# An attention pair's last residual: its bias added in the scores, the sum made by accumulating transfers, and the next layer norm's sums and loads issued in other places

## The chip, the cores and the metric

The kernel runs on one core of one Trainium2 chip. The metric is the device time of one execution in microseconds (us). Everything is float32.

The core has an engine for matrix products (TensorE, "PE" in the profile, with its weight loads as "PEld"), VectorE ("DVE"), ScalarE ("ACT"), GpSimd ("POOL") and SyncE ("SP"). Each takes its own instructions in order. In this kernel SP issues the ordinary loads and stores, and POOL issues the transfers that add to what stands at their destination.

## The reference

The input x is (8, 512, 32, 32): eight batches of 512 channels by 1024 tokens. Two attention layers follow each other.

```python
# layer 0, tokens x channels
xn  = layer_norm(x_flat)                       # over the 512 channels
q, k, v = xn @ Wq.T + bq, xn @ Wk.T + bk, xn @ Wv.T + bv     # 8 heads of 64
out = softmax(q k^T / 8) v
x   = out @ Wo.T + bo + residual
# layer 1, channels x tokens
h   = group_norm(x)                            # 32 groups
q, k, v = wq h + bq, wk h + bk, wv h + bv      # one head of 512
o   = v softmax(q^T k / sqrt(512))^T
return x + (wp o + bp)
```

The change concerns the last line, and the layer norm of a later batch.

## The kernel before, in words

**Batches.** The loop over b = 0 to 7 does, for each batch, layer 0's eight heads (two matmul kinds, s and acc, for each pair of heads), its output product (x_out), layer 1's group norm, layer 1's attention, and then the projections k and q of the next batch's layer 0. The work on batches overlaps: while layer 1 of batch b runs, the sums of the layer norm of batch b+2 are made, and its values are loaded. So batches 6 and 7 have no such work. In the trace a batch takes 352.5 us.

**Layer 1.** Its weights are multiplied together once at the start. With "a" (from wq and wk) one projection qa replaces queries and keys, and with "m" (from wv and wp) the projection vm gives the merged values: the product of vm and the attention weights is already the output wp o. What is left of the biases of values and output is one column for each block of 128 output channels, `bm`.

**Products.** A 2 x 2 block product is done in seven steps instead of eight (`STEPS`, class `Product`). The operands of the steps are blocks such as `11` or `22` and sums of blocks (S1 to S4 of one side, T1 to T4 of the other, made on DVE). Each step multiplies into one of three accumulators in PSUM, called x, y and z. After steps 0, 2 and 3 ACT copies an accumulator out (`copy`, with `plain_shift` L464: tiles u(0, 0), u(0, 1), u(1, 1)), and matmuls may go on in the same accumulator only when that copy is done. After steps 1, 4 and 5 DVE adds an accumulator to the copied tile (`out`, L347). After the last step, number 6, ACT copies the whole block (1, 0). The scores have four such units of 128 keys in their two groups, the projections and the value product two, `r` = 0 and 1. In the profile, s, o, vm and so on name the product: `x_o<-T_p,vm` is a matmul of the value product into x.

**Side work.** Work that isn't tied to one step is queued with `later(...)` in a deque, `side`. Every step of a product ends with `tick`, which takes one piece from it and issues that piece's instructions on whatever engine they need; `until(lambda: not side)` issues all that is left. `nothing` is an empty piece. The order of instructions on PE, ACT, DVE and POOL is therefore fixed by the order in which the program is written out (`manual_schedule(engines=ORDERED)`). SP's loads and stores stand in program order as well, each waiting for its tile. Tiles come from pools that go round: 46 of 128 x 1024 (`big`), 9 of 128 x 512 (`half`), three double banks and two single banks of PSUM.

**Layer 1 of a batch, in order.**
- Group norm gives h1 from x1, layer 0's output. Right after it the four blocks of x1 are stored to DRAM (`put_away`, tiles x_away, 512 KB each), which frees their tiles.
- Projection qa, then the scores: four units. Of each block ACT takes the exponential (L945). DVE adds the exponentials up over the keys (`key_sums`, L968 and L970) and makes the sums of blocks for the value product (`operands`, L981; T3 of the second half is the third of four).
- `fold` adds partitions together by POOL's accumulating transfers: `halve` (L532) adds the upper half of the partitions to the lower, and four small ones (L528) bring them to 32 rows. The result is fold1.
- Projection vm (two units), and load of the weights w_k of the next batch.
- The value product, `Whole.values`. With its first step come, in the program, `ln.sums()` of `LayerNorm(b + 2)` and `inverse` (DVE L536 and others, ACT copies, DVE: 1 / sums, as `rden`).
- After each finished block of this product, `after(i, k)` does: DVE multiplies it by `rden` (L1045), DVE adds the bias column and the stored x1 in one instruction (L1046, `scalar_tensor_tensor`), SP stores the result in out (L1047). The stored x1 comes back in halves, tiles x1r of 128 x 512, 256 KB each, loaded by SP one step ahead (L1041). The very last block of the last batch is done in two halves (`halves`, with its own L1058 that adds the bias to the loaded x1).
- After unit 0 of the value product SP is given the four loads of x for batch b+2 (`load_x`, L152, 512 KB each), and `ln.queue()` puts the rest of that layer norm in the deque, a piece at a time.
- After unit 1: loads of w_q, loads of the stored values v_again, and the projections of k and q.

**The layer norm's sums.** `ln.sums()` brings in the four channel blocks of x with one copying and three accumulating transfers on POOL (L565, tile lns, 512 KB each), then a halve and four folds (L532 and L528, tile fold_mu). The first piece that `ln.queue()` put in the deque is `folded_means`: a transpose of fold_mu on DVE (L536, tile foldm), a reduction (L537) and a scaling (L602). After it come copies on ACT, `expand` (L522), and the centring of x (L629).

The lines at issue, in the program's order:

```python
            o_units[0].step(1)
            ln = LayerNorm(b + 2) if b + 2 < B else None
            if ln:
                ln.sums()
            whole.inverse()
            ...
            o_units[0].rest()
            if ln:
                ln.xt = load_x(b + 2)
                ln.queue()
            o_units[1].rest()
```

## Time and profile before

The median of 3 runs is 2888.99 us (2888.18 to 2889.49). One execution was profiled.

| | |
|---|---|
| profiled execution | 2889.16 us, span 2887.4 us, TensorE clock granted 0.999 |
| PE busy | 2870.4 us, 99% of the span |
| PEld busy (beside PE) | 1386.7 us, 48% |
| DVE busy | 1698.0 us, 59% |
| ACT busy | 1084.2 us, 38% |
| POOL busy | 345.2 us, 12% |
| moved by DMA | 277.17 MB; queue of SP 20.3% of 16 engines' time, queue of POOL 13.2% |
| loads x1r (SP) | 63 of 256 KB, 2.8 us from issue to landing |
| stores x_away (SP) | 32 of 512 KB |
| loads of x (SP) | 32 of 512 KB, 9.5 us |
| lns from x (POOL) | 24 of 512 KB, 5.3 us |
| halving of lns (POOL) | 6 of 256 KB, 8.4 us |
| fold_mu (POOL) | 24 of 64 KB, 2.9 us |
| halving and folds of the pairs' and layer 1's sums (POOL) | 78 of 256 KB, 3.4 us; 312 of 64 KB, 2.4 us |

The span is what the profiler saw, from the first instruction to the last; the time of the execution has 1.8 us more around it. A line of a timeline has the start in us from the beginning of the span, the busy time in us, the engine, the line of the kernel, the operation and its tiles, and in brackets the idle time of the engine before it and what ended that. SPq and POOLq stand for the issue of a DMA by these engines. A group's row has its count, its busy time and the mean of one in ns. Small DMA issues occupy their engine for some 0.8 us each on POOL, and the transfer itself then runs on its own.

### The profile page before, as it was taken

To read this page: it belongs to the slowest core of one execution; us is meant where nothing else is said; L and a number is where in the kernel's file an instruction comes from. 1 tells how busy PE (TensorE), PEld (TensorE's weight loads), DVE (VectorE), ACT (ScalarE), POOL (GpSimd) and SP (SyncE) were. 2 spreads that over 40 slices of the span, in tenths; PEclk is the share of its full clock that TensorE was granted. 3 is DMA by queue.
4 is the path that set the end of the run, shared out by engine and by line. 5 is a ranking of instruction groups with operands and counts; after the bars stand their busy time and mean duration, and the time that the engine had idled before them with its cause. 6 is when DMAs were issued, how large, how long until landed. Compare 5 with 4: busy or idle time off the path is not lost.

```text
span 2887.4 us, 27282 instructions
## 1 busy us (share of the span) xinstructions
PE 2870.4 (99%) x9695; PEld 1386.7 (48%) x9695; DVE 1698.0 (59%) x2181; ACT 1084.2 (38%) x1867; POOL 345.2 (12%) x507
## 2 busy tenths in 40 slices
PE   9999999999999999999999999999999999999998
PEld 4535454355543554445543455434554345543345
DVE  6667354774557645575456755568455674427734
ACT  4462224612256122651226512264222732226331
POOL 2020011200112011120111201011010110002000
PEclk9999999999999999999999999999999999999999
DMA  8134152341613326133252323423244231402302
GB/s 318 45 72 142 34 161 74 68 142 40 181 46 73 135 55 171 44 74 131 63 163 49 88 112 79 148 69 79 102 113 139 63 104 57 124 30 62 117 8 67
DMA packets 110129, 277.17 MB, mean 96 GB/s; under 512 B 16304, under 2 KB 20704, under 8 KB 109984
## 3 DMA queue, kind: packets, MB, share of 16 engines
q1 hardware_dynamic: 81760, 204.51, 20.3%
q0 software_dynamic: 28128, 70.81, 13.2%
q8 instruction: 78, 1.28, 0.2%
q14 instruction: 67, 0.55, 0.1%
q10 hardware_dynamic: 96, 0.02, 0.0%
HBM read 168.85 MB, written 59.24 MB: 79 GB/s over the span
## 4 chain that ended last, share of the span: by engine, by line
PE 99%; DMA 0%; DVE 0%; ACT 0%; issue 0%; SPq 0%; DVEq 0%
PE s L807 15%; PE acc L825 15%; PE x_s L451 8%; PE x_o L459 7%; PE x_v L443 4%; PE x_vm L443 4%; PE x_q L434 4%; PE x_k L434 4%; PE y_s L451 4%; PE x_qa L434 4%; PE x_out L434 4%; PE y_o L459 4%; PE y_v L443 2%; PE y_vm L443 2%; PE y_out L434 2%; PE z_s L451 2%
## 5 line engine op out<-in xcount | busy, mean ns | idle before, releaser
L816 DVE TENSOR_TENSOR sum<-sum,p 128x1024 f32<-128x1024 f32 x384 | 470.4, 1225 | 39.4 <-DVE sum L816 0.9
L810 ACT ACTIVATE p<-s 128x1024 f32<-128x1024 f32 (+1 forms) x608 | 478.8, 990 | 14.4 <-PE s L807 14.4
L807 PE MATMUL s<-q,k 64*128 64x512 f32 x2048 | 448.1, 592 | 0.0
L825 PE MATMUL acc<-p,v_again 128*64 128x512 f32 x1792 | 390.9, 594 | 0.0
L807 PEld LDWEIGHTS s<-q,k 64*128 64x128 f32 x2048 | 195.1, 186 | 251.6 <-issue 158.4
L532 POOL DMA_DIRECT2D sum<-sum x78 | 64.0, 821 | 1719.7 <-DVE sum L970 985.8
L825 PEld LDWEIGHTS acc<-p,v_again 128*64 128x64 f32 x1792 | 126.1, 137 | 261.3 <-issue 238.4
L528 POOL DMA_DIRECT2D fold<-sum x312 | 207.9, 757 | 328.5 <-DMA sum<-sum 199.8
L814 DVE TENSOR_TENSOR sum<-p,p 128x1024 f32<-128x1024 f32 x64 | 78.2, 1222 | 193.6 <-ACT p L810 193.6
L451 PE MATMUL x_s<-S_qa,T_gn 128*128 128x512 f32 x256 | 120.3, 592 | 0.0
L829 ACT COPY o<-acc 128x512 f32<-128x512 f32 x63 | 36.9, 585 | 221.3 <-PE acc L825 221.1
L459 PE MATMUL x_o<-T_p,S_vm 128*128 128x512 f32 x256 | 115.3, 593 | 0.2 <-ACT u(0, 1)_o L464 0.2
L347 DVE TENSOR_TENSOR p<-u(1, 1)_s,x_s 128x512 f32<-128x512 f32 x32 | 22.0, 688 | 128.8 <-PE x_s L451 128.8
L443 PE MATMUL x_vm<-w_m,T_gn 128*128 128x256 f32 x384 | 90.7, 379 | 0.0
L434 PE MATMUL x_qa<-T_gn,w_a 128*128 128x512 f32 x192 | 89.4, 594 | 0.8 <-ACT qa L477 0.8
L434 PE MATMUL x_out<-T_o,w_o 128*128 128x512 f32 x192 | 89.2, 594 | 0.0
L945 ACT ACTIVATE p<-p 128x512 f32<-128x512 f32 x96 | 60.3, 628 | 60.3 <-DVE p L347 60.3
L443 PE MATMUL x_v<-w_v,T_h 128*128 128x256 f32 x336 | 80.0, 381 | 0.0
L464 ACT COPY u(0, 0)_v<-x_v 128x512 f32<-128x512 f32 x16 | 9.4, 585 | 187.5 <-PE x_v L443 187.5
L434 PE MATMUL x_k<-T_h,w_k 128*128 128x512 f32 x168 | 78.9, 592 | 0.0
L434 PE MATMUL x_q<-T_h,w_q 128*128 128x512 f32 x168 | 78.9, 592 | 0.0
L451 PEld LDWEIGHTS x_s<-S_qa,T_gn 128*128 128x128 f32 x256 | 48.6, 190 | 61.2 <-issue 61.0
(334 smaller groups left out, 4252.1 us busy)
## 6 DMA issues: line engine op xcount, KB each, us to landing
sum<-sum POOLq DMA_DIRECT2D x78, 256.0 KB, 3.4
fold<-sum POOLq DMA_DIRECT2D x312, 64.0 KB, 2.4
x<-in_x_dram SPq DMA_DIRECT2D x32, 512.0 KB, 9.5
xr<-in_x_dram SPq DMA_DIRECT2D x64, 256.0 KB, 2.6
x_away<-x SPq DMA_DIRECT2D x32, 512.0 KB
x1r<-x_away SPq DMA_DIRECT2D x63, 256.0 KB, 2.8
v_away<-v SPq DMA_DIRECT2D x28, 512.0 KB, 2.6
v_again<-v_away SPq DMA_DIRECT2D x28, 512.0 KB, 6.5
```

What stands on the lines that cost most here:

```text
L434: nc.tensor.matmul(dst, a[:, k, ts(r, P)], b[:, k, :], start=(opens and k == 0), stop=(k == 1), skip_group_check=True)
L443: nc.tensor.matmul(dst[:, ts(m, CB)], b[:, k, ts(2 * r + m, P)], a[:, k, :], start=(opens and m == 0 and k == 0), stop=(k == 1), skip_grou ...
L451: nc.tensor.matmul(dst, b[:, k, ts(r, P)], a[:, k, :], start=(opens and k == 0), stop=(k == 1), skip_group_check=True)
L459: nc.tensor.matmul(dst, a[:, m, ts(r, P)], b[m // 2][:, m % 2, :], start=(opens and m == 0), stop=(m == NM // 2 - 1), skip_group_check=True)
L528: nc.gpsimd.dma_start(out=f[ts(q + i, BL), :], in_=t[ts(n, BL), ts(i, HB)], accum_op=ALU.add if n else ALU.bypass)
L532: nc.gpsimd.dma_start(out=t[:D, :], in_=t[D:, :], accum_op=ALU.add)
L807: nc.tensor.matmul(parts[i], self.k[m // 4][r, ts(m % 4, P)], self.q[r, :], start=True, stop=True)
L810: nc.scalar.activation(dst, src, AF.Exp, scale=1.0 / float(D) ** 0.5)
L814: nc.vector.tensor_add(self.sum, self.p[0], p)
L816: nc.vector.tensor_add(self.sum, self.sum, p)
L825: nc.tensor.matmul(acc[i * D : (i + 1) * D, :], value_of(self.vt, m, self.c * P + i * D, D), self.p[m][:, ts(i, HB)], start=(m == 0), stop ...
L945: nc.scalar.activation(p, s, AF.Exp, scale=float(C) ** -0.5)
```

## The change

- The bias is added to x1 ahead of its storage: `residual(i, k)` does two activations on ACT (identity with the bias column) on a block of x1, in place, and then SP stores it in x_away. The four pieces are put in the deque behind `query_sums`, so they come at the first steps of the scores, and not right after the group norm.
- For batches 0 to 6, `after(i, k)` has no load x1r and no `scalar_tensor_tensor`: behind the multiplication by `rden`, POOL issues a transfer that adds the stored half block to the tile (256 KB), and SP's store follows that. The last batch still loads x1r and adds it with a plain `tensor_add`, and the last block's L1058 is gone.
- `ln.sums()` is called behind unit 0 of the projection vm, after all that was left in the deque, and ahead of unit 1.
- `load_x(b + 2)` is called behind the first step of the value product and `inverse`.
- `ln.queue()` is called behind the second step of unit 1 and with it two empty pieces; the rest of both units comes after it. Before, it was called when unit 0 was complete.

```diff
@@ -1022,6 +1022,7 @@
 
         def values(self, v):
             b = self.b
+            more = b + 1 < B
             w = {f"{i + 1}{j + 1}": v[i, j].rearrange("p (m o) -> p m o", o=CB) for i in range(2) for j in range(2)}
             shared = {}
 
@@ -1034,16 +1035,19 @@
                     return y[i, k]
 
                 def ahead(n):
-                    if n + 1 not in BLOCK_OF or u.last and n == 5:
+                    if more or n + 1 not in BLOCK_OF or u.last and n == 5:
                         return
                     i, k = BLOCK_OF[n + 1]
                     xr = xr_of[i, k] = half_tile(f"x1r_{b}_{k}_{2 * i + r}")
                     nc.sync.dma_start(out=xr, in_=self.x1[i, k][:, ts(r, HB)])
 
                 def after(i, k):
-                    t, oc, xr = dest(i, k), 2 * i + r, xr_of[i, k]
+                    t, oc = dest(i, k), 2 * i + r
                     nc.vector.tensor_mul(t, t, self.rden[:, ts(k, HB)])
-                    nc.vector.scalar_tensor_tensor(t, t, bm[:, oc : oc + 1], xr, ALU.add, ALU.add)
+                    if more:
+                        nc.gpsimd.dma_start(out=t, in_=self.x1[i, k][:, ts(r, HB)], accum_op=ALU.add)
+                    else:
+                        nc.vector.tensor_add(t, t, xr_of[i, k])
                     nc.sync.dma_start(out=out[b, ts(oc, P), ts(k, HB)], in_=t)
 
                 u = Product(f"o1_{b}_{r}", w, self.p, value_part(r), plain_shift, dest,
@@ -1055,7 +1059,6 @@
                     oc = 2 + r
                     xr = half_tile(f"x1r_{b}_last")
                     nc.sync.dma_start(out=xr, in_=self.x1[1, 0][:, ts(r, HB)])
-                    nc.vector.tensor_scalar(xr, xr, bm[:, oc : oc + 1], None, ALU.add)
                     t = half_tile(f"y_{b}_last")
                     yield
                     both = (slice(0, HB // 2), slice(HB // 2, HB))
@@ -1246,7 +1249,15 @@
                 for n, _ in enumerate(gn.part(slice(None))):
                     meanwhile(n)
             h1 = gn.h
-            x1_away = {ik: put_away(wide(t), f"x1_away_{b}_{ik[0]}{ik[1]}") for ik, t in x1.items()}
+            x1_away = {ik: dram.tile([P, S], F32, tag=f"x1_away_{b}_{ik[0]}{ik[1]}", name=f"x1_away_{b}_{ik[0]}{ik[1]}")
+                       for ik in x1}
+
+            def residual(i, k):
+                t = x1[i, k]
+                for r in range(2):
+                    oc = 2 * i + r
+                    nc.scalar.activation(t[:, r, :], t[:, r, :], AF.Identity, bias=bm[:, oc : oc + 1])
+                nc.sync.dma_start(out=x1_away[i, k], in_=wide(t))
             h1b = operands(h1)
             if more:
                 add_operands(h1b)
@@ -1272,6 +1283,7 @@
             whole = Whole(b, qa, h1b, x1_away)
             s_units = whole.scores()
             whole.query_sums()
+            later(*(lambda ik=ik: residual(*ik) for ik in x1))
             for u in s_units[:2]:
                 u.step(2)
             for u in s_units[:2]:
@@ -1284,26 +1296,29 @@
             later(whole.fold)
             whole.operands(1)
             v_units, vm = project_v(f"vm{b}", wm_now, h1b)
-            for u in v_units:
-                u.rest()
+            v_units[0].rest()
+            ln = LayerNorm(b + 2) if b + 2 < B else None
+            if ln:
+                until(lambda: not side)
+                ln.sums()
+            v_units[1].rest()
             if more:
                 wk_next = load_w("k", b + 1)
             o_units = whole.values(vm)
             check = iter(()) if more else all_checks()
             o_units[0].step(1)
-            ln = LayerNorm(b + 2) if b + 2 < B else None
+            whole.inverse()
             if ln:
-                ln.sums()
-            whole.inverse()
+                ln.xt = load_x(b + 2)
             o_units[0].step(1)
             next(check, None)
             o_units[1].step(2)
             next(check, None)
-            o_units[0].rest()
             if ln:
-                ln.xt = load_x(b + 2)
+                later(*[nothing] * 2)
                 ln.queue()
-            o_units[1].rest()
+            for u in o_units:
+                u.rest()
             if more:
                 wq_next = load_w("q", b + 1)
                 vts = {ik: big_tile(f"v{b + 1}_again_{ik[0]}{ik[1]}") for ik in vn_away}
```

The order of the matmuls is the same in both programs, and so is the order of POOL's transfers apart from the added ones: layer 1's fold stood ahead of the layer norm's sums before, and still does.

## The prediction

> **What bounds the kernel now.** I read the shares of the span and the chain that ended last, then what TensorE waited for, then the timelines of POOL, SP, DVE and TensorE in one batch (batch 3; the program repeats every 352.5 us, eight times). From the page:

> ```profile
> PE 2870.4 (99%) x9695; PEld 1386.7 (48%) x9695; DVE 1698.0 (59%) x2181; ACT 1084.2 (38%) x1867; POOL 345.2 (12%) x507
> ...
> PE 99%; DMA 0%; DVE 0%; ACT 0%; issue 0%; SPq 0%; DVEq 0%
> ```

> TensorE is both the busy engine and the chain. The waits of TensorE (us in total, times, longest):

> ```profile
> PE pst_q L263 <- DMA w_q<-in_L_conv_wq_dram: 5.0, 2, 4.7
> PE pst_k L263 <- DMA w_k<-in_L_conv_wk_dram: 1.2, 1, 1.2
> PE x_qa L434 <- ACT gn L767: 0.8, 1, 0.8
> ...
> PE x_o L459 <- ACT u(0, 1)_o L464: 0.2, 1, 0.2
> ```

> After the first 15 us it waits about 3 us in the whole run. Nothing taken from DVE, ACT or SP can buy more than that, so the question is only whether the change makes a new wait. The timeline of POOL in batch 3 (start, busy, instruction, idle time before it and its releaser) has the chain of the layer norm's sums:

> ```profile
> 1431.11 1.16 POOL L565 DMA_DIRECT2D lns<-in_x_dram  x1
> 1435.70 0.87 POOL L565 DMA_DIRECT2D lns<-in_x_dram  x1 [3.44 <-DMA lns<-in_x_dram]
> ...
> 1452.84 0.82 POOL L532 DMA_DIRECT2D lns<-lns  x1 [4.73 <-DMA lns<-in_x_dram]
> 1462.03 1.05 POOL L528 DMA_DIRECT2D fold_mu<-lns  x2 [8.37 <-DMA lns<-lns]
> 1465.83 1.61 POOL L528 DMA_DIRECT2D fold_mu<-lns  x2 [2.75 <-DMA fold_mu<-lns]
> ```

> Each step waits for the landing of the one before. The 8.37 us is the interesting figure: the halving collided with the loads of x, issued by SP just before it:

> ```profile
> 1449.73 2.81 SPq L152 DMA_DIRECT2D x<-in_x_dram  x4
> ```

> The consumer on DVE, and the matmuls that stand beside it:

> ```profile
> 1462.83 0.69 DVE L347 TENSOR_TENSOR u(1, 1)_o<-u(1, 1)_o,x_o 128x512 f32<-128x512 f32 x1 [8.10 <-PE x_o L459]
> ...
> 1471.64 0.70 DVE L536 STREAM_TRANSPOSE foldm<-fold_mu 64x512 f32<-64x512 f32 x1
> ```

> ```profile
> 1462.56 3.60 PE L459 MATMUL y_o<-p,S_vm 128*128 128x512 f32 x8
> 1465.99 3.60 PE L459 MATMUL x_o<-T_p,vm 128*128 128x512 f32 x8
> ```

> Today foldm runs at 1471.64 without waiting, when all of unit 0 is done. The add at 1462.83 reads x_o, and the last step of unit 0 (1465.99) writes on into x_o, so it must wait for that add.

> [...] The trace has 687 ns from PSUM (L477) and 806 ns from SBUF (L767); I use the trace.

> **The change, part by part.**

> *Residual on ACT.* 8 activations a batch, 64 in all: by L767's 806 ns alone, about 0.72 us each back to back (four of L661 in 2.93 us), 46 us on an engine with 62% idle. They stand among the evacuations of the first score unit. In batch 3: copy u(0,1)_s 1375.07, exp p 1375.55 to 1376.08, then two residuals to 1377.5, then copy u(1,1)_s, which began at 1376.84, now 1377.5 to 1378.1. TensorE's next y_s step starts at 1378.30, its weights half a microsecond before. So 0.1 us a batch, between 0 and 0.4: 0.8 us in eight batches (0 to 3). The other four residuals end near 1381.0, before the exp of x_s due at 1381.94. The four x_away stores move from about 1335 to 1377 to 1382; their first readers on POOL come 80 us later, and what reuses the x buffers comes from 1424. SP's w_k loads behind them are needed at 1486.6. Nothing.

> *DVE.* 56 instructions L1046 at 0.752 us go (42 us), 7 shrink, one L1058 (0.48 us) goes: none is on the chain, so zero gain. SP loses 56 loads x1r of 256 KB; also hidden.

> *Accumulating transfers.* 56 issues on POOL at about 0.8 us (45 us on an engine with 88% idle). They stand behind the four fold_mu, so the first two outputs wait until about 1465. SP's stores wait for them, and behind the stores w_q and v_again. The last ones are ready at 1488.1, plus 0.8 to issue and 3 to land: v_again goes out near 1492.5, not 1489.4, w_q near 1485.5 and 1489; with up to 7 us to land they stand by 1500, and are needed at 1510.6 (x_q) and 1548.8 (acc). The output tiles live longer in the pool of nine half tiles: copy u(0,0) of k (1488.5) needs the store of the second output, gone by about 1475. Nothing, with 10 us of cover.

> *Sums and loads of x.* POOL's order is unchanged: the sums already follow the fold of layer 1, so they start no earlier. What moves is the loads of x, from 1449.7 to behind w_k: the first waits for T3 of p (DVE, 1427.9), the third for a fold, so all four go out between 1428 and 1430.5, just ahead of the first lns. And foldm moves up on DVE, ahead of the add at 1462.83. **DVE now stops at foldm until fold_mu has landed, with that add queued behind it, and TensorE waits for the add.**

> When does fold_mu land? lns to halving 21.7 (1431.11 to 1452.84). The halving and the four folds will be free of x; their price is that of a pair's sums:

> ```profile
> 1556.51 0.80 POOL L532 DMA_DIRECT2D sum<-sum  x1 [1.18 <-DVE sum L816]
> 1560.20 1.06 POOL L528 DMA_DIRECT2D fold<-sum  x2 [2.89 <-DMA sum<-sum]
> 1562.32 1.62 POOL L528 DMA_DIRECT2D fold<-sum  x2 [1.06 <-DMA fold<-sum]
> ```

> that is 3.7 to the first fold, 2.1 to the third, some 3.2 to the fourth's landing: 9.0. Sum 1431.1 + 21.7 + 9.0 = 1461.8, plus c, what the loads of x now cost at the chain's head. The latest landing without a stall: the weights of the last step load at about 1465.5, less the add 0.69, less foldm, reduce and scale 1.6 (1471.64 to 1473.25) and a signal: 1463.1. So batch 3 has 1.3 us to spare. The same sum gives 1.5 and 1.6 for batches 4 and 5, 0.2 and -0.1 for 0 and 1, and 1.0 for 2 (its fourth lns was held 1.4 us by x, which moves). Together 5.5 us of slack in six batches (6 and 7 have no sums).

> c is not in the trace. [...] From above: what x cost the halving, 8.37 + 0.82 - 3.7 = 5.5, less as much x has already gone: 4.7. A single 512 KB load (w_o at 1586.2) cost a halving 2.6. I take 2.3: 6 x 2.3 - 5.5 = 8.3 us of TensorE waits. With ACT's 0.8: **+9.1 us**.

> **Rivals.**
> - *Stall as above, moderate* (c 1.8 to 3.3): +6 to +15 us, likeliest.
> - *Stall, large*: x holds POOL's transfers back as it did the halving, c = 4.7: 6 x 4.7 - 5.5 = 22.7, +23.5 with ACT: 2912.5. For it: 8.37 us in batch 3, 7.6 to 10.1 in the others. Against: part of x is through before lns starts.
> - *No measurable loss*: the four loads of x drain before the first lns needs bandwidth; c at 1.3 or below leaves only batches 0 to 2 late, 2.8 us at most, so 2889 to 2893. It decides at the point where fold_mu lands by 1463.1 in batch 3. [...]
> - *Gain*: the waits of 3 us inside the run would have to go. Nothing in the change touches them.
> - *The change doesn't do what it says*: the sums don't start earlier, as shown; only their consumer and the loads do.

> **How the numbers follow.** The profiled execution took 2889.16 us (span 2887.4 and 1.8 around it), 0.17 above the median of 2888.99; the sum is 2889.0 + 9.1 = 2898. Moderate stall 0.48, large stall or another new wait 0.13, no measurable loss 0.36, gain 0.03. A measurement here can tell 0.2%, 5.8 us. Moderate and large make slower 0.61; the third makes the same 0.36. The range takes in the hidden case and the large stall: 2889 to 2912.

> **What would show it.** In the profile after: TensorE waits on x_o (L459) released by DVE u(1, 1)_o, six times, 0.5 to 3 us each; DVE foldm with idle time before it released by fold_mu; the L565 after the first starting 5.5 to 8 us behind it instead of 4.6; the halving near 3 us of wait instead of 8.4. Wrong if x_o never waits for DVE, if TensorE's waits stand at y_s or at a load instead, or if batch 6, without sums, loses as much as batch 3.

## The result, and the profile after

The changed kernel takes 2918.57 us (median of 4 runs, 2913.68 to 2918.88) against 2889.06 us: a ratio of 1.0099, 95% interval 1.0081 to 1.0116. It is slower, by 29.5 us; the prediction said slower by 9, at most by 23. The profiled execution has a span of 2917.0 us, 29.6 more than before.

The shares of busy time, the chain that ended last, and one group of matmuls (columns: busy us and mean ns; idle time before them and its cause):

```profile
PE 2879.5 (99%) x9695; PEld 1389.8 (48%) x9695; DVE 1654.0 (57%) x2124; ACT 1121.2 (38%) x1931; POOL 394.1 (14%) x563
...
PE 91%; DMA 4%; issue 2%; DVE 1%; POOL 1%; ACT 0%; POOLq 0%; SPq 0%; DVEq 0%; ACTq 0%
...
L459 PE MATMUL x_o<-T_p,vm 128*128 128x512 f32 x120 | 61.8, 664 | 21.2 <-DVE u(1, 1)_o L347 21.2
```

Three things stand here. TensorE's share of the chain falls from 99% to 91%: DMA, issue, DVE and POOL now have pieces of it. One group of matmuls, the last step of the value product, waits 21.2 us for the add u(1,1)_o. And the same group takes 664 ns a matmul, where its neighbours take 592: TensorE is busy 9.1 us longer with the same 9695 matmuls. What TensorE waited for (us in total, times, longest):

```profile
PE x_o L459 <- DVE u(1, 1)_o L347: 21.2, 6, 6.2
PE pst_q L263 <- DMA w_q<-in_L_conv_wq_dram: 5.2, 2, 4.8
```

The first line is new; the others, at the start of the kernel and in the group norms, are within 1 us of those before. Six waits, one for each batch that makes sums for a later layer norm. To see the place, take batch 3 (all of it stands 12.4 us later than before, by what batches 0 to 2 lost). POOL's timeline:

```profile
1429.90 0.80 POOL L532 DMA_DIRECT2D sum<-sum  x1 [122.35 <-DVE sum L970]
...
1443.46 0.80 POOL L528 DMA_DIRECT2D fold<-sum  x1 [2.49 <-DMA fold<-sum]
1445.45 0.77 POOL L528 DMA_DIRECT2D fold<-sum  x1 [1.19 <-DMA fold<-sum]
1446.00 0.81 POOL L565 DMA_DIRECT2D lns<-in_x_dram  x1
1453.30 0.86 POOL L565 DMA_DIRECT2D lns<-in_x_dram  x1 [6.49 <-DMA lns<-in_x_dram]
...
1470.24 0.82 POOL L532 DMA_DIRECT2D lns<-lns  x1 [5.02 <-DMA lns<-in_x_dram]
1474.27 1.05 POOL L528 DMA_DIRECT2D fold_mu<-lns  x2 [3.21 <-DMA lns<-lns]
```

SP's, DVE's and TensorE's:

```profile
1440.43 2.45 SPq L152 DMA_DIRECT2D x<-in_x_dram  x4
```

```profile
1480.11 0.70 DVE L536 STREAM_TRANSPOSE foldm<-fold_mu 64x512 f32<-64x512 f32 x1 [13.74 <-DMA fold_mu<-lns]
1480.85 0.68 DVE L537 TENSOR_REDUCE lnm<-foldm 64x16 f32<-64x512 f32 x1
1481.56 0.17 DVE L602 TENSOR_SCALAR lnm<-lnm 64x16 f32<-64x16 f32 x1
1481.64 0.68 DVE L347 TENSOR_TENSOR u(1, 1)_o<-u(1, 1)_o,x_o 128x512 f32<-128x512 f32 x1
```

```profile
1474.98 3.60 PE L459 MATMUL y_o<-p,S_vm 128*128 128x512 f32 x8
1482.38 5.32 PE L459 MATMUL x_o<-T_p,vm 128*128 128x512 f32 x8 [3.80 <-DVE u(1, 1)_o L347]
```

DVE stands idle for 13.74 us at foldm. The add right behind it could have run 6 us earlier, and TensorE starts 0.06 us after that add. Then eight matmuls take 5.32 us instead of 3.60. The halving now waits 3.21 us where it waited 8.37: the loads of x have left it. They go out at 1440.43, and the last two folds of layer 1 and the first transfer of lns show it.

Counted from the first matmul of the value product in each batch, all six waits follow one line: wait = start of foldm - 25.36 us.

| batch | foldm starts, us behind the first x_o | TensorE's wait | the 8 matmuls after it (3.60 without) |
|---|---|---|---|
| 0 | 27.66 | 2.31 | 5.40 |
| 1 | 29.28 | 3.92 | 5.40 |
| 2 | 28.00 | 2.64 | 3.70 |
| 3 | 29.16 | 3.80 | 5.32 |
| 4 | 31.53 | 6.17 | 5.93 |
| 5 | 27.74 | 2.38 | 3.70 |

The waits are 21.2 us and the slower matmuls 7.9 us (29.5 in the last column, less 6 x 3.60), together 29.1 of the 29.6.

### The profile page after: what moved, and what is told of

Its sections match the earlier page's. It is cut to its first block, busy times and chain, and to the rows that moved or that the text cites. A ratio compares the mean times of both kernels' runs of the same rounds, so it can differ in the third digit from the quotient of the medians.

```text
span 2917.0 us, 27269 instructions
## 1 busy us (share of the span) xinstructions
PE 2879.5 (99%) x9695; PEld 1389.8 (48%) x9695; DVE 1654.0 (57%) x2124; ACT 1121.2 (38%) x1931; POOL 394.1 (14%) x563
## 4 chain that ended last, share of the span: by engine, by line
PE 91%; DMA 4%; issue 2%; DVE 1%; POOL 1%; ACT 0%; POOLq 0%; SPq 0%; DVEq 0%; ACTq 0%
PE s L807 15%; PE acc L825 15%; PE x_s L451 8%; PE x_o L459 6%; PE x_v L443 4%; PE x_q L434 4%; PE x_k L434 4%; PE x_qa L434 4%; PE y_s L451 4%; PE x_out L434 4%; PE y_o L459 3%; PE x_vm L443 2%; PE y_v L443 2%; PE y_out L434 2%; PE y_k L434 2%
## 5 line engine op out<-in xcount | busy, mean ns | idle before, releaser
L816 DVE TENSOR_TENSOR sum<-sum,p 128x1024 f32<-128x1024 f32 x384 | 470.3, 1225 | 39.0 <-DVE sum L816 0.9
L532 POOL DMA_DIRECT2D sum<-sum x78 | 63.5, 814 | 1650.3 <-DVE sum L970 855.9
L528 POOL DMA_DIRECT2D fold<-sum x312 | 208.2, 751 | 343.2 <-DMA sum<-sum 188.4
L459 PE MATMUL x_o<-T_p,S_vm 128*128 128x512 f32 x256 | 115.2, 592 | 0.0
L347 DVE TENSOR_TENSOR p<-u(1, 1)_s,x_s 128x512 f32<-128x512 f32 x32 | 22.0, 687 | 128.8 <-PE x_s L451 122.3
L434 PE MATMUL x_qa<-T_gn,w_a 128*128 128x512 f32 x192 | 89.4, 594 | 0.8 <-ACT qa L477 0.8
L434 PE MATMUL x_out<-T_o,w_o 128*128 128x512 f32 x192 | 89.2, 594 | 0.0
L459 PE MATMUL x_o<-T_p,vm 128*128 128x512 f32 x120 | 61.8, 664 | 21.2 <-DVE u(1, 1)_o L347 21.2
L464 ACT COPY u(0, 0)_v<-x_v 128x512 f32<-128x512 f32 x16 | 9.4, 585 | 187.5 <-PE x_v L443 187.5
L434 PE MATMUL x_q<-T_h,w_q 128*128 128x512 f32 x168 | 79.0, 592 | 0.0
L434 PE MATMUL x_k<-T_h,w_k 128*128 128x512 f32 x168 | 78.9, 592 | 0.0
```

The costliest lines, as they stand in the source:

```text
L434: nc.tensor.matmul(dst, a[:, k, ts(r, P)], b[:, k, :], start=(opens and k == 0), stop=(k == 1), skip_group_check=True)
L459: nc.tensor.matmul(dst, a[:, m, ts(r, P)], b[m // 2][:, m % 2, :], start=(opens and m == 0), stop=(m == NM // 2 - 1), skip_group_check=True)
L528: nc.gpsimd.dma_start(out=f[ts(q + i, BL), :], in_=t[ts(n, BL), ts(i, HB)], accum_op=ALU.add if n else ALU.bypass)
L532: nc.gpsimd.dma_start(out=t[:D, :], in_=t[D:, :], accum_op=ALU.add)
L816: nc.vector.tensor_add(self.sum, self.sum, p)
```

## The experiments

Theory: the whole loss is made at this one place, by the position of foldm on DVE ahead of the add, by a fold_mu that the loads of x delay, and by slow matmuls after each stop. The rivals are that the residual on ACT and the accumulating transfers have a price of their own, and that the chain of sums is too slow even without the loads of x.

**E1: `ln.queue()` back behind unit 0.**

```diff
-                later(*[nothing] * 2)
+            o_units[0].rest()
+            if ln:
                 ln.queue()
-            for u in o_units:
-                u.rest()
+            o_units[1].rest()
```

> The changed kernel with one part undone: ln.queue() stands again behind the whole of unit 0 (no empty pieces), so that DVE meets foldm after the add u(1,1)_o of unit 0. Loads of x, residual on ACT and accumulating transfers stay as changed. Theory (the whole loss is DVE stopped at foldm with that add behind it, and TensorE's slow matmuls after the stop): no wait at x_o, PE busy back from 2879.5 to about 2870, time 2889 (2887 to 2891). Rival (the residual on ACT and the accumulating transfers cost something of their own, so that the 9 us of added PE busy stay): 2895 to 2899.

Measured: 2888.5 us, ratio 1.0002 (0.9993 to 1.0010). DVE in batch 3, the add now first:

```profile
1462.51 0.69 DVE L347 TENSOR_TENSOR u(1, 1)_o<-u(1, 1)_o,x_o 128x512 f32<-128x512 f32 x1 [8.89 <-PE x_o L459]
...
1470.59 0.69 DVE L536 STREAM_TRANSPOSE foldm<-fold_mu 64x512 f32<-64x512 f32 x1
```

No wait for that add is left, and TensorE is busy for 2871.7 us. So the residual on ACT, its later stores, the 56 accumulating transfers and the early loads of x by themselves cost nothing that can be measured (the interval ends at 0.1%, 3 us), and nearly all of the 9 us of added busy time went away with the waits. The rival of own prices falls.

**E4: foldm one step later, behind that add.**

```diff
-                later(*[nothing] * 2)
+                later(*[nothing] * 3)
```

> The changed kernel with three empty pieces ahead of the layer norm's first piece in place of two: foldm moves by one step, from ahead of the add u(1,1)_o of unit 0 to behind it (and ahead of the add u(0,1)_o, whose reader is not TensorE). Theory: fold_mu lands as late as in the changed kernel (foldm starts some 29 us behind the first matmul of the value product), DVE waits for it as long, but TensorE doesn't: 2889 (2888 to 2892). Rival (the late sums hold something else as well, whatever stands behind foldm on DVE): 2900 to 2915, with TensorE's wait at another place.

Measured: 2889.28 us, ratio 1.0004 (0.9995 to 1.0012).

```profile
1462.13 0.69 DVE L347 TENSOR_TENSOR u(1, 1)_o<-u(1, 1)_o,x_o 128x512 f32<-128x512 f32 x1 [8.88 <-PE x_o L459]
...
1466.53 0.70 DVE L536 STREAM_TRANSPOSE foldm<-fold_mu 64x512 f32<-64x512 f32 x1 [2.98 <-DMA fold_mu<-lns]
```

foldm is as late as in the changed kernel (28.0 to 30.9 behind the first x_o in the six batches), DVE still waits for it, and TensorE doesn't. A single empty piece in the queue is worth 29 us: what counts is which instruction stands behind the wait.

**E2: the loads of x behind the four fold_mu, on POOL.**

```diff
-    def load_x(b):
+    def load_x(b, by=nc.sync):
...
-                nc.sync.dma_start(out=t[j, k], in_=x[b, ts(j, CB), ts(k, HB)]...)
+                by.dma_start(out=t[j, k], in_=x[b, ts(j, CB), ts(k, HB)]...)
...
-                ln.xt = load_x(b + 2)
+                ln.xt = load_x(b + 2, nc.gpsimd)
```

> The changed kernel with the four loads of x issued by POOL, behind the four fold_mu, in place of SP at the fold of layer 1; the order on DVE is unchanged. Theory (the loads of x delay fold_mu, by the last folds of layer 1 and by the head of the layer norm's sums): the fold to first lns takes 13.6 us as before, not 16.4; foldm starts about 24 us behind the first matmul of the value product and not 28.9; the point from which TensorE waits is 25.4, so no wait in batches 2 to 5 and at most 1 us in 0 and 1: 2889 to 2892. Rival (the chain of sums is too slow even without the loads of x, by the accumulating transfers or by lns itself): foldm at 27 or later, 2908 to 2919. A new wait for x on DVE could give 2892 to 2897.

Measured: 2888.42 us, ratio 1.0001 (0.9992 to 1.0009). POOL and DVE in batch 3:

```profile
1417.04 0.80 POOL L532 DMA_DIRECT2D sum<-sum  x1 [122.09 <-DVE sum L970]
...
1430.57 1.16 POOL L565 DMA_DIRECT2D lns<-in_x_dram  x1
...
1452.37 0.81 POOL L532 DMA_DIRECT2D lns<-lns  x1 [4.94 <-DMA lns<-in_x_dram]
...
1459.70 3.37 POOL L152 DMA_DIRECT2D x<-in_x_dram  x4
```

```profile
1462.02 0.70 DVE L536 STREAM_TRANSPOSE foldm<-fold_mu 64x512 f32<-64x512 f32 x1 [8.52 <-DMA fold_mu<-lns]
```

With DVE's order of the changed kernel, foldm starts at 23.6 to 25.2 behind the first x_o in five batches, without a wait of TensorE. In batch 4, where no wait was expected, it is 26.14, and TensorE waits 0.79 us: the line of the table again. So the early foldm alone is nearly harmless; it needs the late fold_mu too. The rival of a chain too slow even without the loads of x falls. Set beside this run, the changed kernel's chain of sums can be split (us; the first three columns of numbers are means of the six batches):

| stretch of the chain | this run | changed kernel | cost of the early loads | the same in batch 3 alone |
|---|---|---|---|---|
| layer 1's first halving to the first lns | 13.92 | 16.97 | 3.0 | 2.6 |
| first lns to its halving | 22.01 | 22.68 | 0.7 | 2.4 |
| halving to foldm | 9.76 | 10.30 | 0.5 | 0.2 |

The early loads cost 4.2 us a batch, and most of it at the folds of layer 1. Batch 3 is the one of the six in which lns lost most, and the last row is batch 4 alone (2.5 us there, at most 0.2 elsewhere). The other profiles with all the loads early (E1, E4 and E7) give 2.4 to 3.1 us for the first row and 0.8 to 1.0 for the second.

**E3: the kernel before, with the early foldm alone.**

```diff
             next(check, None)
-            o_units[0].rest()
             if ln:
                 ln.xt = load_x(b + 2)
+                later(*[nothing] * 2)
                 ln.queue()
-            o_units[1].rest()
+            for u in o_units:
+                u.rest()
```

> The kernel before with one part of the change alone: load_x and ln.queue() behind the second step of unit 1 (two empty pieces), so foldm stands ahead of the add u(1,1)_o of unit 0. The loads of x go out some 14 us behind the first matmul of the value product, onto the halving of lns. Theory (position of foldm decides, and the collision with the halving delays fold_mu to 31 to 33): six waits of about 6.5 us, each with 1 to 2 us of slow matmuls after it, 2937 (2925 to 2945), slower than the changed kernel. Rival (the early loads of x alone make the chain late; without them the early foldm is harmless): 2889 to 2895.

Measured: 2934.95 us, ratio 1.0162 (1.0147 to 1.0178). TensorE's wait, and POOL's halving in batch 3:

```profile
PE x_o L459 <- DVE u(1, 1)_o L347: 30.5, 6, 6.2
```

```profile
1476.54 0.82 POOL L532 DMA_DIRECT2D lns<-lns  x1 [4.94 <-DMA lns<-in_x_dram]
1485.11 1.05 POOL L528 DMA_DIRECT2D fold_mu<-lns  x2 [7.75 <-DMA lns<-lns]
```

The edit moves the call of load_x too, but the loads still go out 11.2 us behind the first x_o, as before. Nothing of the residual or of the accumulating transfers on outputs is in this kernel, and it is slower than the changed one. The loads of x meet the halving (7.75 us of wait), foldm starts at 29.7 to 31.5, and each of the six waits is that start less 25.36. They were 5.1 us on average, not the 6.5 expected. So the change's early loads did help, only not enough: counted from E2's mean foldm (24.65), the loads cost the chain 4.2 us in the changed kernel and 5.8 here.

**E6: half of x early.** Two of the four loads stay with SP, two go behind fold_mu on POOL.

```diff
+                by = nc.gpsimd if k == 1 and 2 <= b else nc.sync
-                nc.sync.dma_start(out=t[j, k], in_=x[b, ts(j, CB), ts(k, HB)]...)
+                by.dma_start(out=t[j, k], in_=x[b, ts(j, CB), ts(k, HB)]...)
```

> The changed kernel with the first two of the four loads of x for batches 2 to 7 issued by SP as changed, the other two by POOL behind the four fold_mu. Theory (the delay of fold_mu goes with the bytes of x that compete with the sums): foldm midway between 24.6 and 28.9, about 26.5 us behind the first matmul of the value product, waits of 0.5 to 2 us against the limit of 25.4[...]: 2892 to 2898. Rival 1 (the first loads do the harm, by holding the last folds of layer 1, and the rest is hidden): foldm at 28 to 29, 2908 to 2919. Rival 2 (only the later loads, that meet the first lns, matter): foldm at 25 or below, 2888 to 2890.

Measured: 2899.1 us (2895.53 to 2900.92), ratio 1.0040 (1.0025 to 1.0054), a little over the expected range. The profiled execution took 2895.53; its waits and POOL's timeline in batch 3 (every line number is one higher in this kernel):

```profile
PE x_o L460 <- DVE u(1, 1)_o L348: 5.1, 5, 3.3
```

```profile
1419.25 0.80 POOL L533 DMA_DIRECT2D sum<-sum  x1 [122.35 <-DVE sum L971]
...
1435.04 0.84 POOL L566 DMA_DIRECT2D lns<-in_x_dram  x1
1439.23 0.86 POOL L566 DMA_DIRECT2D lns<-in_x_dram  x1 [3.35 <-DMA lns<-in_x_dram]
```

foldm starts at 26.2 on average of the six, a third of the way from 24.65 (E2) to 28.9, and not midway as expected. Five batches stand at 25.4 to 26.0 and batch 4 at 28.6; there TensorE waited 3.25 us, where 2 at most was expected, and the matmuls after it took 5.11 us instead of 3.60, a slow stretch that was not expected. The other four executions took 3.6 to 5.4 us longer than the profiled one, and no profile shows where. The split is instructive all the same. Layer 1's first halving to the first lns takes 16.46 us on average, so the first two loads alone do most of the harm there (2.5 of 3.0 us). First to second lns takes 3.8 to 4.2 us (5.2 to 7.3 in the changed kernel), so the harm at the head of lns comes from the last two. But lns to halving is 21.1 us here and 22.0 in E2, and the runs don't say what shortened it; that the delay goes with the bytes of x is therefore not shown.

**E5: a stop of TensorE by itself.** The kernel before, with delays put ahead of the add; the multiplications by 1.0 leave the values as they are.

```diff
                 elif i == 4:
+                    for _ in range(self.delay):
+                        nc.vector.tensor_scalar(self.u4, self.u4, 1.0, None, ALU.mult)
                     self.out(1, 1, self.u4, self.x)
...
+                if r == 0:
+                    u.delay = (4, 7, 9, 11, 13, 16, 20, 26)[b]
```

> The kernel before with TensorE's stop made by itself: ahead of the add u(1,1)_o of unit 0 DVE multiplies the 128x512 tile u(1,1)_o by 1.0, 4, 7, 9, 11, 13, 16, 20 and 26 times in batches 0 to 7 (some 0.48 us each, with 2.4 us free). Expected waits of TensorE: about 0, 1, 2, 3, 4, 5, 7 and 10 us, 32 us together. Theory [...]: waits up to 2 us cost only themselves, the six longer ones about 1.7 us more each however long[...]; together 9 us, 2929 (2925 to 2934). Rival 1 (the slow time grows with the wait): the longest wait is followed by 4 us or more of loss, the shortest by some as well, 2933 to 2940. Rival 2 (the slow matmuls of the changed kernel come from DMA traffic and not from the stop): the waits cost only themselves, 2920 to 2922.

Measured: 2907.33 us, ratio 1.0067 (1.0050 to 1.0083); the profiled span is 2903.8. The total missed what every theory expected, by a mistake in the free time: the multiplications need only the copy u(1,1)_o, which is ready well ahead of x_o (in batch 0 they start at 401.60, and the add, which waits for x_o, at 404.42), so some 5.5 us of them are free, not 2.4. Only four batches made TensorE wait (lines L459 and L347 are L462 and L348 in this kernel):

```profile
1818.54 3.70 PE L462 MATMUL x_o<-T_p,vm 128*128 128x512 f32 x8 [0.60 <-DVE u(1, 1)_o L348]
...
2173.32 3.70 PE L462 MATMUL x_o<-T_p,vm 128*128 128x512 f32 x8 [1.99 <-DVE u(1, 1)_o L348]
...
2530.00 5.40 PE L462 MATMUL x_o<-T_p,vm 128*128 128x512 f32 x8 [3.88 <-DVE u(1, 1)_o L348]
...
2874.23 5.68 PE L462 MATMUL x_o<-T_p,vm 128*128 128x512 f32 x8 [6.65 <-DVE u(1, 1)_o L348]
```

These four still answer the question. The two short waits cost little but themselves (0.1 us more); a wait of 3.88 us costs 1.8 more, one of 6.65 us 2.1 more. The last two stand in batches 6 and 7, which have no sums and no loads of x at this place. So the slow matmuls belong to the stop and not to the change's traffic, and a wait 2.8 us longer added only 0.3 us to them.

**E7: the changed kernel again.**

> The changed kernel again, for a second profile of it. Theory [...]: the time of the profiled execution less that of before is the sum of the six waits and 1.7 us for each half-clock stretch, within 1.5 us; the first profile had 21.2 us of waits and four such stretches, one of them two periods long. Rival (a loss of fixed size for each wait): six slow stretches in every execution.

Measured: 2916.78 us, ratio 1.0097 (1.0080 to 1.0114); the profiled span is 2916.7, 29.3 more than before. Its waits are 21.0 us and the slow matmuls after them 7.9, together 28.9. Batches 0, 1 and 4 had a slow stretch, batches 2, 3 and 5 none: the rival of a fixed loss for each wait falls. The slow stretches at half clock last 3.4, 6.8 and 6.8 us, five times 3.41 us together, and 21.0 + 5 x 1.7 = 29.5 us is within the 1.5 us that the expectation allowed. Batch 3 waited 3.18 us and lost nothing more; in the first profile batch 0 waited 2.31 us and lost 1.8. The last section shows how the two waits lay.

## Why the prediction was wrong in size and right in kind

**Right.** The bound, the place, the count and the mechanism: six waits of TensorE on x_o, released by the add u(1,1)_o, DVE idle ahead of foldm for fold_mu, no such wait in batches 6 and 7. The halving's wait near 3 us (3.21), and the first gap of lns longer than 4.6 us (5.2 to 7.3; 5.5 to 8 was expected). The waits themselves, expected at 0.5 to 3 us each, were 2.3 to 6.2. What was costed at nothing cost nothing (E1): DVE's and SP's savings, the accumulating transfers, the later w_q and v_again. TensorE had only 3 us of waits to give back, so nothing was gained.

**Wrong: three terms of the sum.** Between the 9.1 us forecast and the 29.5 measured lie 12.9 us of longer waits (terms 1 and 2) and 7.9 us of slow matmuls (term 3), less the 0.8 us that ACT was to cost and didn't.

1. *c, what the loads of x cost the chain of sums.* It was taken as 2.3 us a batch, 4.7 at most; it was 4.2 on average (E2). The step that failed is where it was looked for: "what the loads of x now cost at the chain's head", the head being the first lns. Between the first lns and the halving the loads cost 0.7 us on average, less than the 1.3 at or below which the prediction saw no measurable loss. But they also run beside the last folds of layer 1, which stand ahead of lns on POOL. These were priced at nothing and lost 3.0 us. Measured from the first x_o, foldm started at 28.9 on average of six batches; the prediction has fold_mu landing at 26.0 (24.6, less a mean slack of 0.9, plus 2.3). Of the 2.9 between them c is 1.9. The other 1.0 is the chain without the loads, 24.65 in E2 where the prediction has 23.7. Most of that is the halving and the folds of lns, put at 9.0 us: in E2 they took 9.76 on average. Two supports of the 2.3 were weak: it has no working of its own below the upper bound of 4.7, and what cost a halving 2.6 us at 1586.2 was not a single load of w_o but two, which SP issued within 1.2 us. The 1.3 was the author's estimate, and not shown: no run here shows how the transfers of SP and POOL shared the DMA engines, only that the last folds of layer 1 lost 2.5 us on average to the first two loads alone (E6).
2. *The limit.* It was 24.6 for the landing; TensorE waits from 25.36 for the start of foldm. The allowance for loading weights before the first matmul wasn't needed: the matmul starts 0.06 us after the add. This was 0.75 us a batch in the other direction. Terms 1 and 2 together: (28.9 - 25.36) x 6 = 21.2 us of waits, where 8.3 stood.
3. *The slow matmuls after a stop*, 7.9 us, are in no term of the prediction, in no rival and in no bound of the range. Without them even c at its upper end gave 2912.5; "stall, large" had 22.7 us of waits, close to the 21.2 measured, and missed the result for want of this term. That it came so near the waits is in part luck: its c was put at lns and not at the folds, and a chain 1.0 us too short and a limit 0.75 us too early nearly cancel.

The residual on ACT was put at 0.8 us; it is nothing. Six of a batch's eight activations stand where they were expected (two ahead of copy u(1,1)_s, four behind it, some 0.64 us each; the first two come one step earlier), and that copy, at 1389.73 in batch 3, was through by 1390.3, ahead of the matmuls at 1390.73.

**Open.** The chain of sums is later in batch 4, less regularly in batch 1, than in the others (31.53 and 29.28 in the table, 30.86 and 30.13 in E7); the runs don't say why. Batch 4 is the latest in E2 too (26.14), so the early loads of x aren't the whole of it. And no kernel here was faster than the one before: E1, E2 and E4 equal it, since TensorE's waits hold no more to be won by these parts.

## What to carry to other kernels

On DVE, which took its instructions in program order here, a consumer that was moved earlier took with it a wait of 13.74 us for its producer: set the producer's landing against the due time of what stands next on that engine, not against the consumer's own need. Loads moved away from one transfer landed on another (the halving waited 3.21 us instead of 8.37, the folds of layer 1 lost 3.0); price such loads along the whole chain, the links ahead of the one you look at too. Where the loads aren't urgent, they can go behind the chain in its own queue, as in E2 (2888.42 us). Where TensorE is the bound, count a stop with the slow matmuls that may follow it (7.9 us beside 21.2 us of waits here).

## What the runs showed of the hardware

```profile
407.07:410.48 3.41, 1.10 (x3) 1.00 0.76 112
410.48:413.89 3.41, 3.41 (x5) 0.50 0.75 165
413.89:417.31 3.42, 3.42 (x9) 1.00 0.83 177
```

```profile
1478.69:1482.10 3.41, 1.91 (x5) 1.00 0.65 61
1482.10:1485.51 3.41, 1.73 (x4) 1.00 0.92 178
```

In the first, 2.31 us of idle time fall into one period (68% of it), and the next runs at half clock: 5 matmuls where the period after it holds 9. In the second, 3.18 us are parted between two periods, 44% and 49%, and the clock stays at 1.00. Over 22 waits in four profiles (two of the changed kernel, E3 and E5) every period that was idle for 68% or more was followed by a half-clock one, and none that ran at full clock and was idle for 56% or less. The longest wait of E6 agrees: 79% of one period, and the next at half clock. A second half-clock period followed in the seven cases where the first was itself idle for 22% to 82%, and in none of the nine where it was idle for 16% or less. So what counted in these waits was the share of a period that stood idle, more than the length of the wait: 2.31 us in batch 0 of the first profile was followed by half clock, 3.18 us in batch 3 of E7 was not. What a half-clock period full of matmuls costs can be estimated as half its length, 1.7 us; behind the wait of 2.31 us the eight matmuls took 1.8 us more (5.40 instead of 3.60).
